# Two graph layers on one core: the third hop as seven products on layer 0's output, the fourth hop six tiles at once, the tests for the pattern in layer 0, first loads in another order

## The chip, the core and the metric

The kernel runs on one core of one Trainium2 chip. The core has TensorE (PE, matrix products), VectorE (DVE), ScalarE (ACT), GpSimd (POOL) and SyncE (SP, which here issues most of the DMAs). The metric is the device time of one execution in microseconds (us); lower is better.

## What is computed

N = 2048 nodes, B = 8 batches, C = 64 features, float32. `adj` is a row-normalised adjacency: each row has the same value at all its nonzero places, 1 over their number.

```python
# layer 0: Chebyshev terms I, A, 2AA-I, weights that depend on the node
w = jnp.einsum('nd,dkio->nkio', embedding, weight)      # D = 16, K = 3
x_g = jnp.einsum('knm,bmc->bnkc', A_stack, x)
out = jnp.einsum('bnki,nkio->bno', x_g, w) + b
x = _layernorm(x + out)
# layer 1: x0, then A x0 and 2 A A x0 - x0, twice with the same adj; one weight
out = jnp.einsum('bnf,fo->bno', x_cat, weight) + bias
x = _layernorm(x + out)
```

So there are four products with `adj`, called hops here: two for layer 0, two for layer 1.

## The kernel before

The nodes lie in 16 tiles of 128. `z[0]`, `z[1]` and `z[2]` hold three versions of the features, each 16 tiles of 128 x 512. A hop works on the pattern of `adj` (a matrix of ones and zeros) and multiplies by the row's value afterwards. The features go into TensorE in two parts, `high` (rounded, ACT) and `low` (the rest, DVE), so every block is multiplied twice. Pattern operands `s` are made from a slab `raw` of `adj`, by `places` (not equal to zero, L197) or by `places_equal` (equal to the row's value, L204), which also counts the places; the counts of the two tests are compared at the end (`check`), and where they differ a general kernel runs instead.

The stages, in the order of the code:

1. **First hop** (`hop_x`, L226): two groups of eight output tiles, 16 slabs each, 512 products of 128x128 by 128x512. ACT counts the places of each `s` by a copy `seen` in bf16 (L438). `put_together` (L390) makes sums of quarters of the pattern, which POOL stores in DRAM (`sums_of`). Ahead of it `first_constants` loads the first features and the bias table on ACT's queue, runs seven idle products and 32 small ones for the bias of each node (`pb`, L145).
2. **Second hop** (`seven_products`, L522): a recursion of one level, seven products of half the size in place of eight, 448 large products. Its result comes out transposed. ACT turns the stored sums into operands (L510); three of the seven products take a quarter of `adj` itself, loaded again and converted on DVE (L197). `put` adds the products together (L540).
3. **Layer 0** (`mix0`, `layernorm`, `project`): per node tile eight PSUM buffers `pm` of 12 products each (L339), 64 rows deep, in pairs that run beside one another; in the trace each of them leaves two records. DVE adds each `pm` to `acc` with the node's embedding as a scalar, four instructions a buffer (L345). Ahead of the last `pm` stand two groups of eight transposes (L265): that of the tile before, for its projection, and that of the next tile's `z[1]`. After the last `pm` comes `project` of the tile before (L358): three weight blocks side by side, 192 columns; ACT writes two of them to `z[0]` and `z[1]` (L365), DVE the third to `z[2]` (L366). `layernorm` goes through DVE (L303, L304), POOL (L306), ACT (L297), DVE (L298), ACT (L284), DVE (L286 to L292) and POOL (L309).
4. **Third hop** (`hop_h`, L226): groups of 4, 8 and 4 output tiles on the projected `z[0]`, 512 products, operands by `places_equal`; the result is added to `z[1]` (`evict`).
5. **Fourth hop**: eight output tiles at once (`hop_g`), then the other eight one by one (`hop_tile`), each followed by its layer norm and store.

The pool `psum` has four buffers of two banks, and all stages draw on it in turn: `bank(name)` takes the next one, whatever it is for. In layer 0 that makes 12 in each tile: seven `pm`, two `pt`, one `pm`, two `pu`. The DMAs and, where `in_order` is set, the work of ACT and DVE keep the order in which the code issues them. In layer 0 `in_order` is empty, and the order on each engine is that of a scheduler. `run` walks through the steps of the hops; each step has parts with a lead (loads four steps ahead, operands two steps ahead), and `todo` holds work of which two pieces follow each step.

Of the kernel before, what the change touches and what calls it, by code (L numbers as in the profile page):

```python
# [8 lines left out]
F32 = mybir.dt.float32  # L9
# [17 lines left out]
WARM = 7  # L27
# [10 lines left out]
def pattern(  # L38
# [20 lines left out]

    nc = tc.nc  # L60
# [13 lines left out]
    rowpool = pool(hops, "frow", 1, side="right")  # L74
    hpool = pool(hops, "fhl", HL, side="right")
# [23 lines left out]
    equal = keep.tile([P, 3 * NT], F32, tag="equal", name="equal")  # L99
# [13 lines left out]
    v = const.tile([P, 3, C], F32, tag="v", name="v")  # L113
# [4 lines left out]
    late_copies = []  # L118
# [7 lines left out]
    def first_constants():  # L126
        load(nc.scalar, z[0][0], x[0].rearrange("n b c -> n (b c)"))
        bias_sb = rawp.tile([P, N // 4 + C], F32, tag="raw", name="bias_sb")
        load(nc.scalar, bias_sb, bias)
        load(nc.scalar, rcol, rcols)  # L130
        eT, b0_sb = bias_sb[:, : N // 4], bias_sb[:, N // 4 :]
        pb = [bank("pb") for _ in range(2)]

        idle = spool.tile([P, 5 * P], BF16, tag="s", name="idle")
        nc.vector.memset(idle, 0.0)
        for _ in range(WARM):
            nc.tensor.matmul(pb[0][:, 0, :], lhsT=idle[:, :P], rhs=idle[:, P:], start=True, stop=True)
        nc.vector.memset(eps, EPS)
        nc.vector.memset(part, 1.0 / C)
        make_identity(nc, ident)  # L140

        for j in range(4):
            for g in range(4):
                q = slice(32 * g, 32 * g + D)
                nc.tensor.matmul(  # L145
                    pb[g // 2][:, g % 2, j * C : (j + 1) * C], lhsT=eT[q, j * P : (j + 1) * P], rhs=b0_sb[q],
                    start=True, stop=True, tile_position=(32 * g, 0),
                )
        for h in range(2):
            to = ebias[:, 8 * h : 8 * h + 8, :].rearrange("p (g t) c -> p g (t c)", g=2)  # L150
            late_copies.append((to, pb[h][:, :, : 4 * C]))

    wl = work2.tile([P, 5, C], F32, tag="t0", name="wl")

    loads = [(pack_sb, pack[:, : NT * D + C]), (wl.rearrange("p k o -> p (k o)"), pack[:, NT * D + C :])]
# [66 lines left out]
    def add_block(accs, s, hl, first, last):  # L222

        for i, a in enumerate(accs):
            for h in range(2):
                nc.tensor.matmul(  # L226
                    a, lhsT=s[:, i * P : (i + 1) * P], rhs=hl[h],
                    start=(first and h == 0), stop=(last and h == 1),
                )
# [3 lines left out]
    def run(steps):  # L233

        got = [{} for _ in steps]
# [64 lines left out]
    def layernorm(src):  # L300
# [8 lines left out]
        nc.gpsimd.tensor_tensor(xc, xc, wide(rsqrt(ss)), ALU.mult)  # L309
        return xc  # L310
# [7 lines left out]
    def mix0(t, tt, between):  # L318
# [4 lines left out]
        for g in range(2):  # L323
# [6 lines left out]
            for dg in range(D // DG):  # L330
                if g == 1 and dg == D // DG - 1:
                    between()
# [15 lines left out]
        return layernorm(acc)  # L348

    def project(t, hT, pus=None):  # L350


        for g in range(2):
            pm = bank("pu") if pus is None else pus[g]
            for i in range(2):
                for j in range(2):
                    q = slice(j * C, (j + 1) * C)
                    nc.tensor.matmul(  # L358
                        pm[:, j, i * 3 * C : (i + 1) * 3 * C], lhsT=hT[q, 2 * g + i, :], rhs=v[q],
                        start=True, stop=True,  # L360
                    )
            got = pm[:, :, : 6 * C].rearrange("p j (i k c) -> p j i k c", i=2, k=3)
            bs = slice(4 * g, 4 * g + 4)
            for s in range(2):
                nc.scalar.copy(bc(s, t)[:, bs, :].rearrange("p (i j) c -> p j i c", j=2), got[:, :, :, 2 - s, :])  # L365
            nc.vector.tensor_tensor(  # L366
                bc(2, t)[:, bs, :].rearrange("p (i j) c -> p j i c", j=2), got[:, :, :, 0, :],
# [12 lines left out]
    S1, S2, S4, S3 = range(4)  # L380
    couple = []
# [11 lines left out]
    def hop_x(g, kk, j):  # L393
        k = kk + KK * j

        def features(_):
            if g == 0 and k > 0:
                load(nc.sync, z[0][k], x[k].rearrange("n b c -> n (b c)"))

        def operands(got):  # L400
            if g == 0 and k == 0:

                s = got["s"] = spool.tile([P, 2, Q], F32R, tag="s", name="s")
                raws = [load_slab(adj[h, 0, :, :Q], [P, Q]) for h in range(2)]
                got["hl"] = halves(z[0][0])
                for h in range(2):
                    ordered(nc.vector.tensor_scalar(s[:, h], raws[h], 0.0, None, ALU.not_equal))
                for to, src in late_copies:
                    ordered(nc.vector.tensor_copy(to, src))
            else:  # L410
                raw = load_slab(adj[:, k, :, g * Q : (g + 1) * Q].rearrange("h m n -> m h n"), [P, 2, Q])
                got["s"] = places(raw)
                got["hl"] = halves(z[0][k])
            couple.append(got["s"])
# [12 lines left out]
        def use(got):  # L427
# [10 lines left out]
            ordered(nc.scalar.activation(seen, s, AF.Copy, accum_out=nonzero[:, i : i + 1]))  # L438
            if last and g == 1:
# [13 lines left out]
    def seven_products(s, to, more):  # L453
# [3 lines left out]
        sums, kept = [], {}  # L457

        def sum_of_y(kk, name):
# [11 lines left out]
            if name == "T2":  # L471
# [4 lines left out]
                return add(y, add(y, quarter(2, 2), quarter(1, 2), ALU.subtract), quarter(1, 1), ALU.add)  # L476
            y = xcpool.tile([P, BC], F32, tag="ln_xc", name="y")
            if name == "T4":
                return add(y, kept[kk // 2][:, kk % 2], quarter(2, 1), ALU.subtract)
# [3 lines left out]
        def step(p, kk):  # L483
# [5 lines left out]
            def y_high(got):  # L489
                hl = hpool.tile([P, 2, BC], F32R, tag="hl", name="hl")  # L490
                got["hl"] = [hl[:, 0], hl[:, 1]]
                if name[0] == "B":
# [6 lines left out]
            def load_sum(got):  # L499
                if isinstance(which, tuple):  # L500
                    return
                raw = got["raw"] = rawp.tile([P, 2, Q], BF16, tag="raw", name="raw")
                load(nc.sync, raw, sums_of[kk, :, :, which, :].rearrange("g m n -> m g n"))

            def operands(got):
                if isinstance(which, tuple):
                    got["s"] = places(slab(kk + KK * which[1], which[0] * HALF, HALF))
# [7 lines left out]
            def use(got):  # L515
# [3 lines left out]
                for i in range(2):  # L519
                    for h in range(2):  # L520
                        for c in range(2):
# [3 lines left out]
                            )  # L525
                if kk < KK - 1:
                    return
                if p < 6:
                    todo.extend([lambda: None] * 4)
                for i in range(2):  # L530
                    for c in range(2):
                        todo.append(lambda i=i, c=c: put(acc[i][:, c], i, c))
                todo.extend(more.get(p, ()))
# [21 lines left out]
            before = [(5, sum_y)] if name[0] != "B" else []  # L555
# [8 lines left out]
    def times_r(t):  # L564
# [6 lines left out]
    pieces = weights()  # L571
    more = {
        1: [lambda: ordered(next(pieces)) for _ in range(13)],
        5: [lambda: times_r(0), lambda: times_r(1)],
    }
    run([hop_x(g, kk, j) for g in range(2) for kk in range(KK) for j in range(2)] + seven_products(1, to_z2, more))
# [13 lines left out]
    def hop_h(g, first, n, k):  # L590
        def operands(got):
            if g == 0 and k == NT - 1:
                project(mixed[0], transpose(mixed[1].rearrange("p b c -> p (b c)"), "hT"))
                layer0.close()
                in_order.append(True)
            i = g * NT + k
            raw = slab(k, first * P, n * P)
            got["s"], got["hl"] = places_equal(raw, first * P, equal[:, i : i + 1]), halves(z[0][k])

        def use(got):  # L600
            s, hl = got["s"], got["hl"]
            if k == 0:
                accs[:] = banks(n)
            add_block(accs, s, hl, k == 0, k == NT - 1)
            if k == NT - 1:
                for i, a in enumerate(accs):
                    evict(z[1][first + i], first + i, a, i % 2)

        return [(2, operands), (0, use)]

    third = [hop_h(g, first, n, k) for g, (first, n) in enumerate(((0, 4), (8, 8), (4, 4))) for k in range(NT)]

    mixed = None
    tt = operands(0)
    for t in range(NT):
        done = {}

        def between():
            if mixed is not None:
                done["hT"] = transpose(mixed[1].rearrange("p b c -> p (b c)"), "hT")  # L620
# [5 lines left out]
        new = t, mix0(t, tt, between)  # L626
        tt = done.get("tt")
        if mixed is not None:
            project(mixed[0], done["hT"])
        mixed = new  # L630
# [27 lines left out]
    EARLY = 8  # L658
    late = []
    ks = [0, 1, 2, 3, 8, 9, 10, 11, 12, 13, 14, 15, 4, 5, 6, 7]  # L660
    hls = {}
    sums = keep.tile([P, 8, B], F32, tag="sums", name="sums")
    late_values = {}

    def hop_g(k):
        def operands(got):
            i = ks.index(k)
            if i == EARLY:
                hops.close()
            if i in (0, EARLY):  # L670
                late.append(pool(ctx, f"flate{i}", 1, reuse_waits="tile"))
            got["s"] = places(slab(k, 0, HALF))
# [3 lines left out]
        def use(got):  # L676
            s, hl = got["s"], hls[k]
            if k == ks[0]:
                accs[:] = banks(8)
            add_block(accs, s, hl, k == ks[0], k == ks[-1])  # L680
            if k == ks[-1]:
                for t, a in enumerate(accs):
                    evict(z[2][t], t, a, t % 2)

        return [(2, operands), (0, use)]

    def hop_tile(t, c):
        def operands(got):
# [3 lines left out]
            got["s"] = places(raw)  # L692

        def use(got):
# [13 lines left out]
            for o in (2 * t - 16, 2 * t - 15):  # L708
                if o < 8:
                    square_sums(bc(2, o), sums[:, o, :])  # L710
            if t == 11:
                late_values["scales"] = rsqrt(sums.rearrange("p t b -> p (t b)"))
            if t >= 12:
                for o in (2 * t - 24, 2 * t - 23):
# [9 lines left out]
    run(third + [hop_g(k) for k in ks] + [hop_tile(t, c) for t in range(8, NT) for c in range(2)])  # L724
# [324 lines left out]
```

## Time and profile before

| | |
|---|---|
| time, median of 3 runs | 839.27 us (838.78 to 840.99) |
| profiled execution | 841.55 us, its span 839.8 us, mean granted clock 0.996 |
| PE busy | 823.0 us (98%) |
| DVE busy | 607.4 us (72%) |
| ACT busy | 224.8 us (27%) |
| POOL busy | 128.4 us (15%) |
| DMA | 96.56 MB, 115 GB/s over the span |
| first hop | 7.97 to 127.0 us |
| second hop | to 228.56 us |
| layer 0 | to 594.21 us |
| third and fourth hop | to 828.46 us |

The span runs from the first to the last instruction; the execution's time also holds what lies around it (1.75 us here). The borders of the stages are read from the chain of waits. In the timeline each row is a start, a length, an engine, a line of the code, an operation, what it writes and reads, and how many instructions the row joins; in brackets is idle time of the engine just before it, and what ended it. A length ends when the result is written, so lengths of neighbours overlap a little, and the distance between starts says what an instruction costs its engine.

### The profile page before, as it was taken

How to read it: one execution, taken by the hardware profiler on the slowest of the kernel's cores; microseconds unless marked ns; L12 is line 12 of the kernel's file. 1: busy time of each engine (PE TensorE's matmuls, PEld its weight loads, DVE VectorE, ACT ScalarE, POOL GpSimd, SP SyncE). 2: the span in 40 equal slices, each digit the busy share in tenths (PEclk: the TensorE clock that was granted, in tenths of full speed). 3: DMA queues.
4: the chain of work that ended last, by engine and by line, in shares of the span. 5: the costliest groups of instructions: out<-in, count | busy, mean ns of one | idle time of the engine just before them, and what ended most of it. 6: DMA issues, size and time to landing. Idle time of an engine off the chain costs nothing.

```text
span 839.8 us, 14386 instructions
## 1 busy us (share of the span) xinstructions
PE 823.0 (98%) x5609; PEld 732.7 (87%) x5609; DVE 607.4 (72%) x1256; ACT 224.8 (27%) x427; POOL 128.4 (15%) x130
## 2 busy tenths in 40 slices
PE   8999999999999999999999999989999999999995
PEld 6888888888888999999999999989888878888884
DVE  5868758757877988888788888788867567534662
ACT  4445446773101111111111111111331132401210
POOL 0100000001641111111111110120101020102133
PEclk9999999999999999999999999999999999999998
DMA  9976786458400000000000000030256327544462
GB/s 327 399 237 197 234 288 202 145 152 280 126 14 3 13 14 14 14 14 14 14 13 14 14 13 14 25 102 2 75 182 192 93 73 245 172 140 123 136 179 92
DMA packets 57181, 96.56 MB, mean 115 GB/s; under 512 B 3984, under 2 KB 28816, under 8 KB 56976
## 3 DMA queue, kind: packets, MB, share of 16 engines
q1 hardware_dynamic: 52064, 82.39, 31.0%
q0 software_dynamic: 2304, 8.39, 3.1%
q10 hardware_dynamic: 2736, 4.76, 1.5%
q8 instruction: 47, 0.77, 0.4%
q14 instruction: 30, 0.25, 0.1%
HBM read 82.94 MB, written 12.58 MB: 114 GB/s over the span
## 4 chain that ended last, share of the span: by engine, by line
PE 93%; DVE 4%; DMA 1%; issue 1%; ACT 0%; POOL 0%; ACTq 0%; DVEq 0%; POOLq 0%
PE pm L339 35%; PE acc L226 35%; PE accT L522 12%; PE a L226 7%; DVE acc L345 3%; PE pu L358 2%; PE pt L265 1%; DMA raw<-in_adj 1%; DMA bias_sb<-in_bias 1%; DVE s L204 0%; POOL got L315 0%; PE pb L145 0%; ACT L284 0%; POOL xc L306 0%; DVE s L303 0%
## 5 line engine op out<-in xcount | busy, mean ns | idle before, releaser
L226 PE MATMUL acc<-hl,s 128*128 128x512 f32 x1280 | 294.8, 392 | 0.0
L226 PEld LDWEIGHTS acc<-hl,s 128*128 128x128 f32 x1280 | 241.7, 189 | 52.1 <-issue 0.8
L345 DVE SCALAR_TENSOR_TENSOR acc<-pm,pack_sb,acc 128x256 f32<-128x256 f32 x512 | 246.3, 483 | 41.2 <-PE pm L339 19.8
L339 PE MATMUL pm<-w,xt 64*128 64x256 f32 x1024 | 160.8, 378 | 3.9 <-DVE acc L345 3.8
L339 PE MATMUL pm<-w,t 64*128 64x256 f32 x1024 | 159.7, 376 | 0.2 <-ACT t L267 0.2
L339 PE MATMUL pm<-w,z 64*128 64x256 f32 x1024 | 159.6, 376 | 0.0
L339 PEld LDWEIGHTS pm<-w,xt 64*128 64x128 f32 x1024 | 107.8, 187 | 6.4 <-issue 3.3
L339 PEld LDWEIGHTS pm<-w,t 64*128 64x128 f32 x1024 | 110.5, 187 | 2.0 <-ACT t L267 0.6
L339 PEld LDWEIGHTS pm<-w,z 64*128 64x128 f32 x1024 | 110.4, 187 | 1.5
L197 DVE TENSOR_SCALAR s<-raw 128x1024 fp32r<-128x1024 f32 x87 | 67.4, 776 | 59.6 <-PE acc L226 49.7
L522 PE MATMUL accT<-s,hl 128*128 128x512 f32 x448 | 101.7, 389 | 0.0
L522 PEld LDWEIGHTS accT<-s,hl 128*128 128x128 f32 x448 | 84.1, 188 | 17.5
L208 ACT CAST hl<-z 128x512 fp32r<-128x512 f32 (+1 forms) x120 | 66.8, 578 | 116.5 <-PE acc L226 108.7
L212 DVE TENSOR_TENSOR hl<-z,hl 128x512 fp32r<-128x512 f32 (+1 forms) x120 | 81.5, 681 | 17.3 <-ACT hl L208 14.4
L204 DVE SCALAR_TENSOR_TENSOR s<-raw,rrow 128x512 fp32r<-128x512 f32 (+1 forms) x48 | 46.8, 978 | 26.3 <-PE acc L226 24.6
L267 ACT COPY hT<-pt 128x512 f32<-128x512 f32 x16 | 9.4, 585 | 204.4 <-PE pt L265 204.4
L306 POOL TENSOR_TENSOR xc<-acc,s 128x512 f32<-128x512 f32 x16 | 16.7, 1042 | 280.2 <-DVE s L304 280.2
L226 PE MATMUL a<-hl,s 128*128 128x512 f32 x256 | 58.5, 390 | 0.0
L226 PEld LDWEIGHTS a<-hl,s 128*128 128x128 f32 x256 | 48.0, 188 | 10.0
L255 POOL TENSOR_TENSOR z<-z,got 128x512 f32<-128x512 f32 x12 | 18.9, 1594 | 154.6 <-ACT got L254 154.6
L325 POOL TENSOR_TENSOR acc<-z,ebias 128x256 f32<-128x256 f32 x32 | 27.0, 865 | 85.9 <-ACT hl L208 84.3
L510 ACT CAST s<-raw 128x1024 fp32r<-128x1024 bf16 x32 | 33.6, 1051 | 12.0 <-ACT hl L208 11.3
(87 smaller groups left out, 476.1 us busy)
## 6 DMA issues: line engine op xcount, KB each, us to landing
raw<-in_adj SPq DMA_DIRECT2D x103, 512.0 KB, 4.5
raw<-in_adj SPq DMA_DIRECT2D x34, 256.0 KB, 3.0
sums_of<-z POOLq DMA_DIRECT2D x16, 512.0 KB, 4.6
raw<-sums_of SPq DMA_DIRECT2D x32, 256.0 KB, 2.8
xt<-in_xT SPq DMA_DIRECT2D x16, 256.0 KB, 2.6
out<-got ACTq DMA_DIRECT2D x16, 256.0 KB, 2.0
z<-in_x SPq DMA_DIRECT2D x15, 256.0 KB, 8.3
w<-in_w SPq DMA_DIRECT2D x3, 512.0 KB, 5.4
```

Of the source, the lines that this page charges most:

```text
L197: ordered(nc.vector.tensor_scalar(s, raw, 0.0, None, ALU.not_equal))
L204: ordered(nc.vector.scalar_tensor_tensor(s, raw, 0.0, r, ALU.add, ALU.is_equal, accum_out=count))
L208: ordered(nc.scalar.copy(to[0], src))
L212: ordered(nc.vector.tensor_tensor(to[1], src, to[0], ALU.subtract))
L226: nc.tensor.matmul(a, lhsT=s[:, i * P : (i + 1) * P], rhs=hl[h], start=(first and h == 0), stop=(last and h == 1),)
L255: ordered(nc.gpsimd.tensor_tensor(to, to, got, ALU.add))
L325: nc.gpsimd.tensor_tensor(part.rearrange("p (j i) c -> p j i c", j=2), bc(0, t)[:, 4 * g : 4 * g + 4, :].rearrange("p (i j) c -> p j i c", ...
L339: nc.tensor.matmul(pm[:, j, i], lhsT=tt[k][q, 2 * g + i, :], rhs=w[k][q, ds, :], start=(k == 0), stop=(k == 2),)
L345: nc.vector.scalar_tensor_tensor(part, pm[:, :, :, d, :].rearrange("p j i c -> p (j i) c"), emb_sb[:, t, dd : dd + 1], part, ALU.mult, ALU.add
L358: nc.tensor.matmul(pm[:, j, i * 3 * C : (i + 1) * 3 * C], lhsT=hT[q, 2 * g + i, :], rhs=v[q], start=True, stop=True,)
L510: ordered(nc.scalar.copy(s, got["raw"]))
L522: nc.tensor.matmul(acc[i][:, c], lhsT=hl[h][:, i * P : (i + 1) * P], rhs=S[:, c * 512 : (c + 1) * 512], start=(kk == 0 and h == 0), stop=( ...
```

## The change

- **First loads.** The two halves of the first slab are issued on SP first, then each `x` tile just ahead of its slab. The bias table moves to the `loads` list, loaded at the start of the first hop's second group; its products (`node_bias`) run in the second hop. Twelve idle products in place of seven. In the first step all products with `high` come ahead of those with `low`.
- **Quarters kept.** ACT stores every second `seen` tile, bf16, to `quarters` in DRAM. In `seven_products`, two of the three products on a plain quarter load it from there, and ACT converts it. The sums `T4` are made during the fourth product.
- **Tests in layer 0.** `test(t)`: a slab of the second half of `adj` is compared with the row's value and counted, one 1024-wide DVE instruction per tile ahead of the third `pm` (tile 8 has a second one ahead of its seventh; tile 15 has none, and issues operands of the third hop's first two steps).
- **Projection.** `layernorm` writes back to `z[0]`; `project` applies two weight blocks (128 columns).
- **Third hop.** `seven_products` on layer 0's output, into `zT` (transposed). The third weight block is applied to `zT` afterwards (`weigh`, 128 products of 64 columns) and the result is added to `z[1]` (`add_weighed`). The last tile is transposed and projected inside its first product.
- **Fourth hop.** Six output tiles at once in `hop_g`, operands by `places_equal` (768 wide); ten tiles one by one, the first two of them with `places_equal` as well.

```diff
-WARM = 7
+WARM = 12
...
     def first_constants():
         load(nc.scalar, z[0][0], x[0].rearrange("n b c -> n (b c)"))
-        bias_sb = rawp.tile([P, N // 4 + C], F32, tag="raw", name="bias_sb")
-        load(nc.scalar, bias_sb, bias)
         load(nc.scalar, rcol, rcols)
...
-    loads = [(pack_sb, pack[:, : NT * D + C]), (wl.rearrange("p k o -> p (k o)"), pack[:, NT * D + C :])]
+    loads = [(bias_sb, bias), (pack_sb, pack[:, : NT * D + C]), (wl.rearrange("p k o -> p (k o)"), pack[:, NT * D + C :])]
...
     def add_block(accs, s, hl, first, last):
 
-        for i, a in enumerate(accs):
-            for h in range(2):
...
+        order = [(i, h) for i in range(len(accs)) for h in range(2)]
+        if first:
+            order.sort(key=lambda ih: ih[1])
...
-    def layernorm(src):
+    def layernorm(src, to):
...
-        nc.gpsimd.tensor_tensor(xc, xc, wide(rsqrt(ss)), ALU.mult)
-        return xc
+        xc, r = (a.rearrange("p (g m) c -> p g m c", g=2) for a in (xc, wide(rsqrt(ss))))
+        nc.gpsimd.tensor_tensor(to, xc, r, ALU.mult)
...
     def project(t, hT, pus=None):
...
-                        pm[:, j, i * 3 * C : (i + 1) * 3 * C], lhsT=hT[q, 2 * g + i, :], rhs=v[q],
+                        pm[:, j, i * 2 * C : (i + 1) * 2 * C], lhsT=hT[q, 2 * g + i, :], rhs=v[q, 0:2, :],
...
+            nc.scalar.copy(z1_part, got[:, :, :, 1, :])
             nc.vector.tensor_tensor(
-                bc(2, t)[:, bs, :].rearrange("p (i j) c -> p j i c", j=2), got[:, :, :, 0, :],
+                z2_part, got[:, :, :, 0, :],
                 bias1.unsqueeze(1).unsqueeze(1).to_broadcast([P, 2, 2, C]), ALU.add,
...
     def hop_x(g, kk, j):
         k = kk + KK * j
 
-        def features(_):
-            if g == 0 and k > 0:
-                load(nc.sync, z[0][k], x[k].rearrange("n b c -> n (b c)"))
+        def features(got):
+            if g == 0 and k == 0:
+                got["raws"] = [load_slab(adj[h, 0, :, :Q], [P, Q]) for h in range(2)]
...
             ordered(nc.scalar.activation(seen, s, AF.Copy, accum_out=nonzero[:, i : i + 1]))
+            if j == 1:
+                ordered(nc.scalar.dma_start(out=quarters[kk, :, :, g, :], in_=seen))
...
             def operands(got):
-                if isinstance(which, tuple):
-                    got["s"] = places(slab(kk + KK * which[1], which[0] * HALF, HALF))
+                if which == (0, 0):
+                    got["s"] = places(slab(kk, 0, HALF))
                 else:
...
-    third = [hop_h(g, first, n, k) for g, (first, n) in enumerate(((0, 4), (8, 8), (4, 4))) for k in range(NT)]
...
+    def weigh(ts, pairs, bs):
+        for n, t in enumerate(ts):
+            to = columns(pairs, n, bs)
+            for i in range(2 * len(bs)):
+                for j in range(2):
+                    q, block = slice(j * C, (j + 1) * C), 2 * bs[0] + i
+                    nc.tensor.matmul(
+                        to[:, j, i * C : (i + 1) * C], lhsT=zT[t // 8, t // 4 % 2][q, t % 4, block * P : (block + 1) * P],
+                        rhs=v[q, 2, :], start=True, stop=True,
+                    )
...
+    third = seven_products(0, to_zT, sums3, {
+        (0, 4): [last_transposed],
+        (0, 5): [lambda: in_order.append(True)],
+        (0, 6): [last_projected],
+        4: half_weighed(1, 0), 5: half_weighed(0, 1),
+    }, wait=2)
...
+    def test(k):
+
+        raw = slab(k, HALF, HALF)
+        return lambda: tc.keep_in_program_order(
+            nc.vector.scalar_tensor_tensor(
+                raw, raw, 0.0, rrow[:, HALF:], ALU.add, ALU.is_equal, accum_out=equal[:, k : k + 1]
+            )
+        )
...
+        at = {(1, 3): [between]}
+        if t < NT - 1:
+            at[0, 2] = [test(t)]
+        else:
+            at[0, 1], at[0, 3] = [lambda: early(0)], [lambda: early(1)]
+        if t == NT // 2:
+            at[1, 2] = [test(NT - 1)]
+        mix0(t, tt, at)
...
-    EARLY = 8
+    G = 6
...
-            got["s"] = places(slab(k, 0, HALF))
+            got["s"] = places_equal(slab(k, 0, G * P), 0, equal[:, NT + k : NT + k + 1])
...
-    run(third + [hop_g(k) for k in ks] + [hop_tile(t, c) for t in range(8, NT) for c in range(2)])
+    run(third + [hop_g(k) for k in range(NT)] + [hop_tile(t, c) for t in range(G, NT) for c in range(2)], third_got)
```

## The prediction

> **What bounds the kernel now.** First the busy times and the chain of waits, for the engine that sets the end; then the chain in order of time, for stage borders; then the timeline of VectorE (DVE) and TensorE (PE) inside one tile of layer 0, where the change adds work.
>
> ```profile
> PE 823.0 (98%) x5609; PEld 732.7 (87%) x5609; DVE 607.4 (72%) x1256; ACT 224.8 (27%) x427; POOL 128.4 (15%) x130
> PE 93%; DVE 4%; DMA 1%; issue 1%; ACT 0%; POOL 0%; ACTq 0%; DVEq 0%; POOLq 0%
> ```
>
> The chain is nearly all PE. Its pieces give the stages: first hop 7.97 to 127.0 us, second hop to 228.56, layer 0 to 594.21, third and fourth hop to 828.46, tail to 839.8. DVE's 72% hides layer 0. One of its tiles, first on DVE, then on PE (start us, us, engine, line):
>
> ```profile
> 385.59 2.04 DVE L345 SCALAR_TENSOR_TENSOR acc<-pm,pack_sb,acc 128x256 f32<-128x256 f32 x4 [0.92 <-PE pm L339]
> 387.55 0.41 DVE L366 TENSOR_TENSOR z<-pu,pack_sb 128x256 f32<-128x256 f32 x1
> 387.88 0.68 DVE L303 TENSOR_REDUCE s<-acc 128x8 f32<-128x512 f32 x1
> 388.59 0.17 DVE L304 TENSOR_TENSOR s<-s,part 128x8 f32<-128x8 f32 x1
> 388.68 0.42 DVE L366 TENSOR_TENSOR z<-pu,pack_sb 128x256 f32<-128x256 f32 x1
> 390.64 0.69 DVE L298 TENSOR_REDUCE ss<-sq 128x8 f32<-128x512 f32 x1 [1.55 <-ACT sq L297]
> ...
> 392.52 14.73 DVE L345 SCALAR_TENSOR_TENSOR acc<-pm,pack_sb,acc 128x256 f32<-128x256 f32 x28
> ```
>
> ```profile
> 404.79 0.43 PE L265 MATMUL pt<-ident,xc 64*128 64x64 f32 x8
> 405.04 0.44 PE L265 MATMUL pt<-ident,z 64*128 64x64 f32 x8
> 405.29 0.68 PE L339 MATMUL pm<-w,xt 64*128 64x256 f32 x4
> ```
>
> A tile lasts 22.57 us. DVE is occupied for all but the 0.92 before the last product pm7: 28 additions at 14.73/28 = 0.526, so the sixth product (pm5) is drained at 392.52 + 24 x 0.526 = 405.14. PE starts pm7 at 405.29. There are four PSUM buffers, and two transposes lie between pm6 and pm7, so pm7 takes pm5's buffer: the ring is closed to 0.15 us[...]. DVE's 0.92 is no slack: it is the time in which PE makes pm7 after DVE has freed its buffer. The trace has a test of this, where extra DVE work fell into tile 14:
>
> ```profile
> 546.79 0.69 DVE L204 SCALAR_TENSOR_TENSOR s<-raw,rrow 128x512 fp32r<-128x512 f32 x1 [1.33 <-DMA raw<-in_adj]
> ...
> 549.41 1.53 DVE L204 SCALAR_TENSOR_TENSOR s<-raw,rrow 128x512 fp32r<-128x512 f32 x1 [0.20 <-DMA raw<-in_adj]
> ...
> 550.88 1.20 DVE L204 SCALAR_TENSOR_TENSOR s<-raw,rrow 128x512 fp32r<-128x512 f32 x1
> ...
> 552.01 1.20 DVE L204 SCALAR_TENSOR_TENSOR s<-raw,rrow 128x512 fp32r<-128x512 f32 x1
> ```
>
> The first with its wait added 1.95 us; the other three stretched the gap between L304 and L298 from 1.96 to 4.0, so 2.05 more: 4.0 in all. PE's transposes at 540.76 and 590.02 lie 49.26 apart where two tiles are 45.14: 4.12 lost. DVE work here costs its full length.
>
> **The Trainium skill.** TensorEngine Tiling (Array Packing), PSUM Bottleneck: tiling speeds up TensorE, not the evacuation of PSUM. The trace agrees: 64-row products in pairs, and DVE without room. Perfetto Trace Analysis, Optimization Strategy: a gap repeating on the engine that should be full can mean too few buffers; the 0.92 on DVE, in each tile at one place, is its twin here. TensorE: Matmul & The Clock Gate, Part 1: cold PE runs at 1.2 GHz until some 3.4 us of work. The seven idle products took 3.17 us (0.425 apart) and the first 15 of the first hop 6.44, against 0.227 each later.
>
> **The change part by part.**
>
> *Start.* SP issues the two adjacency pieces ahead of x, and the bias load, which the chain waits for until 5.94, leaves the front with its 32 small products (1.98 us). Twelve idle products end at 1.25 + 12 x 0.425 = 6.35; the operands should be there by about 5.5 (the first x was cast at 4.68, the pieces are issued 0.9 earlier). The hop starts 1.6 earlier. It lost 119.05 - 512 x 0.2268 = 2.9 to the cold clock; without the gap I take 1.9 of that as gained. The bias products return in the second hop at 32 x 0.031 (the 64-column pace of L265): +1.0. Sum -2.5, bounds -4.5 and -1. The 16 new stores of quarters from ACT add 36 GB/s to 319 in the first half of the hop, where DMA is 0.89 busy; buffers run ahead and PE never waits there, so nothing. If that cover goes, PE waits; 2 us at most. ACT pays 16 issues of about 0.45 in a hop where it is half idle. In the second and third hop ACT's copy (1.05) replaces DVE's (0.78) in two products; ACT then needs 1.45 of a step's 1.81: nothing. The y sums of T4 move earlier under the same cover.
>
> *Layer 0.* (a) A 1024-wide test per tile, on DVE's queue between the second and third product, ahead of pm5. L204's 1024-wide row starts at 640.40 and its successor at 641.55: 1.15. The slab for it is issued a tile ahead on SP. (b) In the compiled order both L375 (was L366) stand ahead of the reduction; before, the second lay inside the wait for ACT and was free: +0.34. Each of tiles 1 to 14 pays 1.49: 20.9. Tile 0 pays nothing: DVE waits about 0.5 for each of its products. The second test of tile 8 lies after pm5, beside PE's pm7: +0.3. (c) project narrows from 192 to 128 columns: 16 records from 0.081 to 0.055, 0.42 a tile; behind a ring that DVE closes it saves nothing. (d) Tile 14's loss and 0.34 in tile 8 go: -4.4. (e) Tile 15 has no test, but early operands of the third hop: eleven 256-wide instructions at 0.35 fill an idle 1.9 and add 2.0, two more and four conversions at 0.61 add 3.1, L375 0.34. It has one transpose fewer, so pm7 takes pm4's buffer and the 0.9 goes: against 22.32 now, +4.8. Sum 20.9 + 0.3 - 4.4 + 4.8 = **+21.6**.
>
> *Third and fourth hop.* 64 large products fewer (448 for 512) at 0.2268: -14.5. 128 products of 64 columns, two records each as for L339 (3072 for 1536): 256 x 0.0306, the pace of L265 with the same stationary shape, +7.8; above, 0.062 as the bias records (1.98/32), +15.9; below, 64 columns at the slope of L358 to L339, 0.027, +6.9. Last tile's projection -0.6. Six tiles at once instead of eight leaves 512 products. DVE has 1.6 of a 2.7 us step there. The last tile's normalised result, about 7 us after its last addition, is wanted after five steps (9.1): hidden, and if not, the transposes hold PE by the difference. Sum -7.3. The tail stays.
>
> Total -2.5 + 21.6 - 7.3 = **+11.8**. The profiled execution took 841.55 (span 839.8), giving 853.4; it stood 2.3 above the median of the runs, so I predict 839.27 + 11.8 = **851.1**.
>
> **Rivals.**
> 1. DVE has room in layer 0 and PE sets the pace (faster). Place: the ring at pm7. If the test fitted into the 0.92 and the waits for ACT (1.5), tiles would take 22.57 - 0.42: -2.5 - 6.3 - 4.4 - 7.3 = -20.5, 818.8. It decides once a tile's extra falls below 1.49 - 11.8/14 = 0.65. For it: tests stand at 72% DVE, and casts in tiles 2 to 5 did vanish in that wait. Against: the test stands ahead of pm5, not in the wait, and tile 14 paid in full. 0.08.
> 2. Half of it: (b) free and part of a test hidden, start and tile 15 at their good ends: near 839. 0.05.
> 3. More than forecast: tests stretch beside GpSimd to 1.5 as at 549.41 (+5), or the small products are paced as the bias records (+8): 856 to 859. 0.15, on my side.
> 4. The change isn't what it says: the compiled order shows the tests, 128 small products and 448 large ones, so none.
>
> **Numbers.** About 0.3% (2.5 us) can be told from no change. My forecast with rival 3 has 0.87, so slower 0.87, same 0.05, faster 0.08. Low: no (b), best start, easier tile 15: 851.1 - 4.8 - 2 - 3 = 841. High: rival 3, 859.
>
> **What would show it.** Right: transposes in layer 0 some 24.05 apart, PE waiting 1 to 2 us a tile for DVE ahead of pm7, layer 0 near 387 us long, third and fourth hop near 227. Wrong: spacing near 22.2 without waits on PE (rival 1); third hop longer than 110 with small products 0.06 apart (rival 3); a first hop that starts after 7 us or shows waits for DMA.

## The result, and the profile after

The change makes the kernel slower: 865.84 us (median of 4 runs, 865.01 to 866.33) against 839.44 us before (median of 4). The ratio is 1.0308, interval 1.0295 to 1.0321. The forecast had the direction (slower, 0.87) and less than half of the size: 851.1 us, with 859 as the upper end. The profiled execution of the kernel after took 865.87 us with a span of 863.6 us, 23.8 us more than the span before.

From the page of the kernel after, the busy times and then the shares of the chain of waits:

```profile
PE 830.1 (96%) x5806; PEld 728.9 (84%) x5806; DVE 603.0 (70%) x1311; ACT 267.5 (31%) x464; POOL 109.8 (13%) x121
...
PE 62%; DVE 25%; issue 8%; POOL 2%; ACT 2%; DVEq 0%; POOLq 0%
```

Two things are to be seen. DVE now holds a quarter of the chain, where it held 4%: layer 0 goes over to it. And PE is busy for 7 us more, although it was given less to do in large products (1920 for 1984); that line can't be explained by layer 0.

One tile of layer 0 after, from the timeline, first DVE, then PE:

```profile
403.98 3.15 DVE L353 SCALAR_TENSOR_TENSOR acc<-pm,pack_sb,acc 128x256 f32<-128x256 f32 x6
407.05 1.22 DVE L704 SCALAR_TENSOR_TENSOR raw<-raw,rrow 128x1024 f32<-128x1024 f32 x1
...
408.19 10.43 DVE L353 SCALAR_TENSOR_TENSOR acc<-pm,pack_sb,acc 128x256 f32<-128x256 f32 x20
419.52 1.52 DVE L353 SCALAR_TENSOR_TENSOR acc<-pm,pack_sb,acc 128x256 f32<-128x256 f32 x3 [0.90 <-PE pm L347]
...
424.77 0.69 DVE L306 TENSOR_REDUCE ss<-sq 128x8 f32<-128x512 f32 x1 [1.89 <-ACT sq L305]
```

```profile
414.60 0.69 PE L273 MATMUL pt<-ident,z 64*128 64x64 f32 x16
416.62 0.70 PE L347 MATMUL pm<-w,xt 64*128 64x256 f32 x4 [1.33 <-DVE acc L353]
```

The test (L704) occupies DVE from 407.05 to 408.19, 1.14 us. The wait for PE ahead of the last additions is still there (0.90, before 0.92), and PE now waits 1.33 in each tile for a buffer. The ring of the forecast is as it was, and the test lengthens it. The stages, from the starts of their first products:

| | before | after | difference | forecast |
|---|---|---|---|---|
| start, first and second hop, to layer 0's first product | 228.8 | 232.7 | +3.9 | -2.5 |
| layer 0 | 365.3 | 379.0 | +13.7 | +21.6 |
| third and fourth hop | 235.5 | 241.9 | +6.4 | -7.3 |
| tail | 10.1 | 10.0 | -0.1 | 0 |

So layer 0 is cheaper than forecast, and everything around it dearer. The first row is the clue: the first hop's 512 products are the same in both kernels, start 1.9 us earlier after the change, and end only 0.4 us earlier. Large products that nobody had touched ran at another pace. Here is PE in two stretches that hold nothing but large products (columns: stretch; its length, PE busy and number of instructions; granted clock; DMA share; GB/s), before and after:

```profile
140.00:220.00 80.00, 80.00 (x354) 1.00 0.63 198
...
770.00:830.00 60.00, 60.00 (x266) 1.00 0.47 141
```

```profile
140.00:220.00 80.00, 80.00 (x345) 1.00 0.47 150
...
770.00:830.00 60.00, 60.00 (x263) 1.00 0.59 178
```

The clock is full, no instruction waits, DMA moves less in the second hop, and still 345 products fit where 354 did. From start to start a large product took 0.2267 us throughout before; after, it took 0.2343 in the first hop, 0.2333 in the second and third, and in the fourth 0.2342 in one half of the products and 0.2268 in the other. Over the 1920 large products this is 11.5 us more than at the forecast's 0.2268.

### The profile page after: what moved, and what is told of

Read it like the earlier page. It is cut to its first block, busy times and chain, and to the rows that moved or that the text cites. A ratio compares the mean times of both kernels' runs of the same rounds, so it can differ in the third digit from the quotient of the medians.

```text
span 863.6 us, 14814 instructions
## 1 busy us (share of the span) xinstructions
PE 830.1 (96%) x5806; PEld 728.9 (84%) x5806; DVE 603.0 (70%) x1311; ACT 267.5 (31%) x464; POOL 109.8 (13%) x121
## 4 chain that ended last, share of the span: by engine, by line
PE 62%; DVE 25%; issue 8%; POOL 2%; ACT 2%; DVEq 0%; POOLq 0%
PE accT L546 24%; DVE acc L353 20%; PE acc L230 14%; PE pm L347 10%; PE a L230 6%; PE accT L230 5%; PE accT L656 2%; POOL xc L314 1%; DVE ss L306 1%; ACT sq L305 1%; DVE z L375 1%; DVE s L311 1%; PE first L134 1%; POOL got L323 0%; ACT ln_sd L292 0%
## 5 line engine op out<-in xcount | busy, mean ns | idle before, releaser
L546 PE MATMUL accT<-s,hl 128*128 128x512 f32 x896 | 211.1, 396 | 1.2 <-DVE z L375 0.8
L546 PEld LDWEIGHTS accT<-s,hl 128*128 128x128 f32 x896 | 167.6, 188 | 42.5 <-DVE z L375 1.2
L230 PE MATMUL acc<-hl,s 128*128 128x512 f32 x512 | 120.7, 397 | 0.0
L534 ACT CAST s<-raw 128x1024 fp32r<-128x1024 bf16 x96 | 100.9, 1051 | 51.8 <-ACT hl L210 36.8
L230 PEld LDWEIGHTS acc<-hl,s 128*128 128x128 f32 x512 | 96.5, 189 | 24.1 <-DVE z L438 0.5
L214 DVE TENSOR_TENSOR hl<-z,hl 128x512 fp32r<-128x512 f32 (+1 forms) x96 | 53.3, 562 | 34.7 <-ACT hl L210 31.9
L210 ACT CAST hl<-z 128x256 fp32r<-128x256 f32 (+1 forms) x96 | 47.3, 510 | 66.3 <-PE acc L230 32.9
L230 PE MATMUL accT<-hl,s 128*128 128x512 f32 x192 | 45.5, 395 | 0.0
L230 PEld LDWEIGHTS accT<-hl,s 128*128 128x128 f32 x192 | 35.8, 188 | 8.1
L453 ACT ACTIVATE seen<-s 128x1024 bf16<-128x1024 f32 x32 | 33.7, 1053 | 16.8 <-DMA quarters<-seen 16.8
```

The source lines that it names most:

```text
L210: ordered(nc.scalar.copy(to[0], src))
L214: ordered(nc.vector.tensor_tensor(to[1], src, to[0], ALU.subtract))
L230: nc.tensor.matmul(accs[i], lhsT=s[:, i * P : (i + 1) * P], rhs=hl[h], start=(first and h == 0), stop=(last and h == 1),)
L534: ordered(nc.scalar.copy(s, got["raw"]))
L546: nc.tensor.matmul(acc[i][:, c], lhsT=hl[h][:, i * P : (i + 1) * P], rhs=S[:, c * 512 : (c + 1) * 512], start=(kk == 0 and h == 0), stop=( ...
```

## The experiments

The theory of the pace came from addresses, which stand in the compiled programs and in no view of a profile. The pool `keep`, which lies first in SBUF, grew by 352 bytes (`v` moved in; `equal`, `sums` and the columns of its square root shrank), and all that lies to the left of the free space moved with it: the pattern tiles `s`, and those feature tiles `hl` of the fourth hop that lie on that side. The `hl` of the first three hops are laid from the right end and stayed. (A large product takes 128 columns of one and 512 of the other; `s` is the stationary one in the first and fourth hop, `hl` in the seven products. "Pair" below means the start addresses of both.) The first idea was the remainder modulo 64.

**e1, e2: 32 bytes.** One unused tile at the start of `keep`, in the kernel after (e1) and before (e2):

```diff
+    keep.tile([P, 8], F32, tag="pad", name="pad")
     rcol = keep.tile([P, NT], F32, tag="rcol", name="rcol")
```

> The changed kernel with one unused tile of 32 bytes per partition at the start of its first SBUF pool, so that the stationary tiles s of the large products lie at 32 modulo 64 bytes, as the moving tiles hl do; without it s lies at 0. No instruction is added or removed. Theory A (where stationary and moving operand stand at different remainders modulo 64 bytes, a large product takes .234 us in place of .2267): the large products of hops 1 to 3 go back to about .227 and those of hop 4 to about .228, 1408 products x .0070 + 384 x .0025 = -10.8, and with the same at other places up to -13.5 us: 852 to 855. Rival B (the large products are slow because of the new order of loads, or because the kernel is a longer one): no change, 865 to 866.

> The kernel before with the same 32 bytes, which puts its s at 0 modulo 64 bytes while the hl of hops 1 to 3 stay at 32. Theory A: its 1472 large products of hops 1 to 3 go from .2267 to about .234, +10.5 us, hop 4, whose moving tiles move along with s, stays: about 850. If the place of s alone decides and not the pair, hop 4 is slower too: +13.5, about 853. Rival B: no change, 839.

e1 took 863.91 us, ratio to before 1.0283 (1.0266 to 1.0300), so 2 us of the 11.5 came back. e2 took 848.76, ratio 1.0093 (1.0074 to 1.0112): 8.5 us lost by 32 unused bytes. The stretches again, e1 and then e2:

```profile
140.00:220.00 80.00, 80.00 (x346) 1.00 0.49 153
...
770.00:830.00 60.00, 60.00 (x264) 1.00 0.60 184
```

```profile
140.00:220.00 80.00, 80.00 (x345) 1.00 0.60 189
...
770.00:830.00 60.00, 60.00 (x267) 1.00 0.43 138
```

e2 settles that addresses do it: apart from them nothing differs from the kernel before, and the second hop has the pace of after, while the fourth hop, where `s` and `hl` moved together, kept 267. So rival B is out. But e1 was a miss: modulo 64 its pairs agree everywhere, and it stayed slow. Put beside each other, all the traces agreed on another number:

| kernel | `s` mod 256 | `hl` of hops 1 to 3 | pace | `hl` of hop 4 | pace |
|---|---|---|---|---|---|
| before | 224 | 224 | 0.2267 | 224 | 0.2267 |
| after | 64 | 224 | 0.2343, 0.2333 | 224, then 64 | 0.2342, 0.2268 |
| e1 | 96 | 224 | 0.2324 | 224, then 96 | 0.2325, 0.2274 |
| e2 | 0 | 224 | 0.2333 | 0 | 0.2268 |

**e5, e9: 160 and 256 bytes.** The same unused tile with 40 elements in the kernel after (e5), and with 64 in the kernel before (e9).

> The changed kernel with an unused tile of 160 bytes in place of the 32 of e1, so that s and every hl leave the same remainder modulo 256 bytes (224). In the traces so far each pair of equal remainders modulo 256 ran at .2267 to .2274 (before 224/224, e2's hop 4 0/0, after's second half of hop 4 64/64, e1's 96/96), each unequal pair at .2324 to .2342, e1's 96/224 too, which are equal modulo 64 and 128. Theory A2 (equal remainders modulo 256, or a multiple of it, decide): all 1920 large products at .2267, the 11.6 us that after's spend over that go: 854. Theory A1 (64 decides, and something else held e1 up): as e1, 864. Rival B: no change, 866.

> The kernel before with an unused tile of 256 bytes: s leaves 224 modulo 256 as the hl of hops 1 to 3 do, but modulo 512 s now leaves 224 and they 480. Theory M256 (the remainder modulo 256 decides): every large product stays at .2267, no change, 839 to 840. Theory M512 (modulo 512): the 960 of hops 1 and 2 and the 512 of hop 3 go to .232 to .234, +8 to +10, about 848.

e5 took 855.81 us, ratio 1.0188 (1.0167 to 1.0209): 10.0 us less than the kernel after, of the 11.5 that the pace should give back (in its trace the first hop starts 0.2 later and PE waits 0.7 for DVE in it). e9 took 839.58, ratio 0.9995 (0.9985 to 1.0005). The same stretch of the second hop and one of the fourth, e5 and then e9 (in e9 the fourth hop ends inside the last stretch):

```profile
140.00:220.00 80.00, 80.00 (x354) 1.00 0.51 158
...
770.00:830.00 60.00, 60.00 (x267) 1.00 0.56 172
```

```profile
140.00:220.00 80.00, 80.00 (x355) 1.00 0.61 194
...
770.00:830.00 60.00, 57.87 (x256) 1.00 0.46 137
```

Theory A2 holds: with equal remainders modulo 256 every large product is back at 0.227. e9 shows that 256 is enough, since modulo 512 its pairs differ. Why the memory or the array behaves so is not shown; no run here looks inside a product.

**e4, e10: what the small products cost.** In the kernel after, the 128 products of `weigh` leave 256 records. e4 takes half of the stationary columns, e10 half of the moving ones.

```diff
-to[:, j, i * C : (i + 1) * C], lhsT=zT[...][q, t % 4, block * P : (block + 1) * P], rhs=v[q, 2, :]
+to[: P // 2, j, i * C : (i + 1) * C], lhsT=zT[...][q, t % 4, block * P : block * P + P // 2], rhs=v[q, 2, :]    # e4
+to[:, j, i * C : i * C + C // 2], lhsT=zT[...][q, t % 4, block * P : (block + 1) * P], rhs=v[q, 2, : C // 2]    # e10
```

> The changed kernel with 64 instead of 128 stationary columns in each of the 256 small products that apply the weights in the third hop; this leaves out their term for half of the nodes. Theory L (loading 128 fp32 columns of a row group takes about .11 us, two row groups in turn, so .060 per product): half the columns, .030 to .035 per product, 15.2 goes to 8 or 9 us, -6 to -7: 859. Rival M (the price is that of the 64 moving columns in fp32, or a fixed one of each record): 15.2 stays, 865 to 866.

> The changed kernel with 32 instead of 64 moving columns in each of the 256 small products that apply the weights in the third hop; this leaves out their term for half of the features. Theory L (as in e4: loading 128 stationary columns in fp32 sets their price): 15.2 us stay, 865 to 866. Rival M (moving columns count as well, so that e4's saving was that of a smaller product as a whole): .030 to .045 per product, -4 to -7.5, 858 to 862.

From the timelines of PE, the first 64 records and the large products behind them, in the kernel after, in e4 and in e10:

```profile
695.05 3.79 PE L656 MATMUL accT<-v,zT 64*128 64x64 f32 x64
698.77 7.50 PE L546 MATMUL accT<-s,hl 128*128 128x512 f32 x31
```

```profile
694.29 2.08 PE L656 MATMUL accT<-v,zT 64*64 64x64 f32 x64
696.30 10.07 PE L546 MATMUL accT<-s,hl 128*128 128x512 f32 x42
```

```profile
695.70 3.76 PE L656 MATMUL accT<-v,zT 64*128 64x32 f32 x64
699.39 6.96 PE L546 MATMUL accT<-s,hl 128*128 128x512 f32 x22
```

From start to start 64 records take 3.72 us after, 2.01 in e4, 3.69 in e10: 0.058, 0.031 and 0.058 each. e4 took 858.64 us (1.0219, 1.0198 to 1.0239), 7.2 less than after; 256 x 0.027 is 6.9. e10 took 869.0 (1.0339, 1.0314 to 1.0364); in its profiled run the granted clock stood at 0.98 from 615 to 800 us, as an estimate 185 x 0.02 = 3.7 us, about the 3.2 by which it lies above after. So from 64 moving columns down to 32 the price hangs on the stationary columns and not on the moving ones, as theory L has it. The Trainium skill, "TensorE: Matmul & The Clock Gate", LDWEIGHTS, says that a load takes P / 1.2 ns for P columns, whatever the rows, which makes 107 ns for 128; Part 3 of the page adds that loads overlap with running products only where the row group differs. With two row groups side by side that is, as an estimate, 0.053 a record for 128 columns and 0.027 for 64; measured are 0.058 and 0.031, each some 0.005 above. The trace's own records of these loads last longer than the page's 107, 188 ns for 128 columns (after) and 135 for 64 (e4), but they lie 53 apart, as 64 / 1.2 would have it. The transposes (L273) have the same form by the profile, 64*128 by 64x64, and take 0.031 a record; their loads last 139 ns, nearly as short as those of 64 columns. Why a transpose loads faster is open.

**e3, e7: where a test can hide.** e3 moves it from behind the additions of the second product to the place in `layernorm` where DVE waits 1.9 us for ACT; e7 moves it behind those of the sixth product (`pm5`), beside which PE makes the last one.

```diff
-            at[0, 2] = [test(t)]
+            at["wait"] = [test(t)]      # e3: run in layernorm, behind L312
+            at[1, 2] = [test(t)]        # e7
```

> The changed kernel with the test of a tile of layer 0 (1.15 us of DVE) moved from between the additions of products 1 and 2 to the place in layernorm where DVE waits 1.9 us for ACT. Theory (layer 0 goes round the ring DVE addition, PE product, DVE addition, and each test lengthens it by its own time; in the wait it is free): the period of a tile goes from 23.71 back to 22.57, 15 x 1.14 = -17 us, about 849. If DVE's port, shared with POOL during layernorm, stretches the work there by .3 a tile: -12, about 854. Rival (DVE has room in the ring, so the +14.7 of layer 0 came from the order of products and weights): no change, 865.

> The changed kernel with the test of a tile in layer 0 moved behind the additions of product 5, beside which PE makes product 7; there DVE waits .9 us for PE a tile. Theory R (any DVE work inside the ring of additions lengthens the period by itself less the wait it fills): 1.15 - .9 = .25 a tile, period about 22.8, -13: 853. Rival (the wait of .9 is made by DVE's own earlier additions through the banks, so that it moves along): period stays 23.7, 866.

e3 took 865.95 us (1.0305, 1.0288 to 1.0322): nothing gained, the period went from 23.71 to 23.61. It looks like the rival's result, and is not. DVE and POOL in e3, then POOL in the kernel after:

```profile
398.94 1.22 DVE L706 SCALAR_TENSOR_TENSOR raw<-raw,rrow 128x1024 f32<-128x1024 f32 x1
...
401.75 0.69 DVE L306 TENSOR_REDUCE ss<-sq 128x8 f32<-128x512 f32 x1 [1.59 <-ACT sq L305]
```

```profile
399.16 1.89 POOL L316 TENSOR_TENSOR xc<-acc,s 128x512 f32<-128x512 f32 x1 [17.97 <-DVE s L312]
```

```profile
399.32 1.04 POOL L314 TENSOR_TENSOR xc<-acc,s 128x512 f32<-128x512 f32 x1 [18.92 <-DVE s L312]
```

The wait on DVE is ended by ACT, but what fills it first is POOL's subtraction; with the test beside it that takes 1.89 in place of 1.04, and DVE still waits 1.59 afterwards. The 0.85 goes straight into the ring, and 0.19 more is lost because the 28 additions take 14.73 again, as without a test among them, and not 14.54: of 1.14 that leaves a gain of 0.1 a tile. The Trainium skill has the rule, "SBUF — State Buffer", Who interferes with whom: a DVE instruction with two inputs in SBUF contends with a GpSimd instruction that reads SBUF; the test has two (`raw`, `rrow`), and the 0.85 agrees. The expectation of e3 had 0.3 for this.

e7 took 855.6 us (1.0183, 1.0156 to 1.0211), 10.2 less. The period is 22.91, so theory R holds. PE around the last product of a tile:

```profile
410.02 0.69 PE L273 MATMUL pt<-ident,z 64*128 64x64 f32 x16
411.24 0.70 PE L347 MATMUL pm<-w,xt 64*128 64x256 f32 x4 [0.54 <-DVE acc L353]
```

PE waits 0.54 for the buffer instead of 1.33, and DVE's own 0.90 is gone, since the test fills it.

**e8: no tests in layer 0.** e5 with the tests in the third hop, where DVE is half idle.

```diff
+    for k in range(NT):
+        at, to = divmod(9 + 2 * k, KK), divmod(11 + 2 * k, KK)
+        more3.setdefault(at, []).append(lambda k=k: load_test(k))
+        more3.setdefault(to, []).insert(0, lambda k=k: test(k))
```

> e5 with the 16 tests taken out of layer 0 and put into the third hop, one every second step of its seven products, each with its load two steps earlier; there DVE is busy 5 to 6 tenths. Theory (PE bounds hop 3, DVE has room): layer 0 back to a period of 22.57, -17, and nothing added: with A2 854 - 17 = 837, at or a little below before. Rival (the tests delay the additions that free the third hop's banks, or their loads the ones that products wait for): up to +18 in hop 3, 854.

It took 842.7 us (median of 20 runs; 1.0033, 1.0026 to 1.0041), 13.1 less than e5. Layer 0 shrank by 13.4 and the third and fourth hop stayed at 237.4, so the tests cost nothing there. Two rows of DVE in the third hop:

```profile
625.94 0.41 DVE L215 TENSOR_TENSOR hl<-y,hl 128x256 fp32r<-128x256 f32 x1
626.27 1.22 DVE L690 SCALAR_TENSOR_TENSOR raw<-raw,rrow 128x1024 f32<-128x1024 f32 x1
```

It missed the 837 by 5.7 us: e5 was already 1.8 above its own expectation, and the period became 22.76 and not 22.57, 2.7 over 14 tiles, and the expected 17 had counted 15 tiles that pay 1.14 for a test, where 14 do. In its tiles the 28 additions take as long as before the change; the 0.19 is the second L375 (here L376), which now lies ahead of the reduction (L312):

```profile
391.31 14.73 DVE L354 SCALAR_TENSOR_TENSOR acc<-pm,pack_sb,acc 128x256 f32<-128x256 f32 x28
```

**e6: the start alone,** in the kernel before.

```diff
-WARM = 7
+WARM = 12
...
+    loads = [(bias_sb, bias), (pack_sb, ...
...
+        if first:
+            order.sort(key=lambda ih: ih[1])
...
+        (0, 3): [lambda: node_bias(sums2[1]), ...
```

> The kernel before with the new start alone: adjacency ahead of features, bias terms moved into the second hop's first product, 12 warming products, products of the first block ordered by half; layer 0, the third and the fourth hop and all addresses of s and hl as before. Theory (the step of the forecast was right, and only the slower large products hid it): -2.5 (1.6 earlier, 1.9 of cold clock, +1.0 of bias in hop 2), about 837. Rival (the loads that now come later make a later wait): no change, 839 to 840.

838.95 us (median of 20 runs) against 839.8 (39 runs), ratio 0.9988 (0.9981 to 0.9995): a gain of 0.85 us, a third of the forecast. Its trace alone would have misled, for its span is 2.9 shorter than that of the kernel before. PE in the first hop's beginning, before, in e9 (whose instructions are those of before) and in e6:

```profile
8.00:10.00 2.00, 2.00 (x5) 1.00 0.86 268
10.00:12.00 2.00, 2.00 (x6) 1.00 1.05 389
12.00:14.00 2.00, 2.00 (x7) 1.00 1.05 399
```

```profile
8.00:10.00 2.00, 2.00 (x7) 0.56 0.90 291
10.00:12.00 2.00, 2.00 (x7) 0.59 1.04 402
12.00:14.00 2.00, 2.00 (x10) 1.00 1.05 397
```

```profile
8.00:10.00 2.00, 2.00 (x11) 1.00 1.05 398
10.00:12.00 2.00, 2.00 (x10) 1.00 1.05 389
```

In the trace on which the forecast rested, PE ran at little more than half its pace until about 14 us; in e9's until 12, with the hop starting at 7.17 instead of 7.90 and ending at 124.9 instead of 126.9. This is read off the numbers of products: the clock column shows it in e9 (0.56 and 0.59) and reads 1.00 in the trace of before. That one execution was 2 us slower at its start than e9's, and the forecast booked this as a gain of the change. e6 is the fastest kernel of the study, by 0.1% over before; which of its parts gave that is not separated.

## Why the prediction was right and wrong

**Right: the mechanism in layer 0.** DVE's 0.92 is no slack where the test was put, DVE work in the ring costs about its length, and nothing hides the test. The trace shows PE waiting 1.33 us in each tile ahead of the last product (forecast: 1 to 2), and e8 shows that without tests 13.4 us of layer 0 go. Rival 1 is out, and e3 and e7 show why no simple place was free: the wait for ACT is a wait for POOL, too, which the test holds up; only the 0.9 behind `pm5` takes it, and e7 got 10.2 back there, of the 13.1 that e8 gained by taking the tests out. (The forecast's own lines had that wait for ACT, 1.55, beside its sentence that DVE is occupied for all but the 0.92.)

**Mis-sized: layer 0, +21.6 against +13.7.** A tile of 1 to 14 pays 1.14 and not 1.49. e8 parts it: order (b) costs 0.19 (forecast 0.34), and the test 0.95 (forecast 1.15). The test itself has 1.14 in the trace; the rest comes back because the 28 additions take 14.54 in the tiles with a test, 14.73 without; why they do is not shown. This is -4.9 over 14 tiles. Of the other terms, (d) gave -3.9 for -4.4, and (e) +3.4 for +4.8 (tile 15 takes 25.76 where it took 22.32); the third hop starts 1.4 earlier against the last layer norm, for which the forecast had taken 0.6 off the third hop.

**Failed: the price of the small products.** The step took 0.0306 from the transposes with the same shape and put the sum at +7.8. They cost 0.059, 15.2 in all. That the transposes don't load as other products do stood in the profile of before (after the first stroke: busy us, mean ns of one load):

```profile
L358 PEld LDWEIGHTS pu<-v,hT 64*128 64x128 f32 x256 | 22.5, 187 | 0.4 <-ACT hT L267 0.4
...
L265 PEld LDWEIGHTS pt<-ident,xc 64*128 64x128 f32 x128 | 7.3, 138 | 1.1 <-issue 0.4
```

Rival 3 had this end (+8 above the forecast), for a wrong reason: the 0.062 of the bias records belongs to the slow start of that one execution (in e9's trace the same 32 records take 1.12 us, 0.035 each). The nearest true row was L358 with its 128 stationary columns, but extrapolated along the moving columns to 0.027 it led below. With few moving columns the price no longer falls: it is 0.081 with 192 (L358), 0.056 with 128 (L366 in the kernel after), 0.058 with 64 and with 32. So the third hop's saving of 64 large products, 14.5, is paid out again in small ones.

**Failed: a term that was not there.** The forecast priced every large product at 0.2268, because that was its pace throughout the trace of before, and so put the effect of the new addresses at nothing. The diff changes the size of a pool, and with it the remainder of `s` modulo 256: +11.5 us, of which e5 got 10.0 back. No view of the kernel before could show it; the compiled program's addresses could have raised the question, and only e2 and e5 answered it.

**Failed: the start,** -2.5 against -0.85 (e6), as above: the slow first products of one execution were booked as the kernel's. The forecast knew that this execution stood 2.3 above the median of the runs, and still added the whole gain read off it to the median.

The errors in their order: +11.5 addresses, +7.4 small products, -7.9 layer 0, +1.7 start, +1.2 for waits of the third hop's first product for layer 0's last additions and projection, which the trace names and the forecast left out, +0.6 for the last tile's projection, which went from layer 0 and not from the third hop. Together 14.5 of the 14.7 by which 865.84 lies above 851.1. The range ended at 859 because it was made of the ends of the terms that the forecast had; the largest error had no term.

Where the expected gain went: with the addresses mended and the tests out of layer 0 (e8), the change still stands 2.9 us above the kernel before. Its seven products save 14.5 and the weights cost 15.2.

## What to carry to other kernels

Ahead of any story about the changed part, compare the pace of an instruction that the change didn't touch: here it gave 11 us at a glance. Take the price of a new product from one with the same stationary columns and the same kind of operation, and see, in the records of its loads too, whether its load or its moving columns set it, before drawing a line through other sizes. An engine's wait is free room only if nothing that the wait stands for is held up by the new work: here POOL's subtraction was.

## What was not expected of the hardware

- A large product (128x128 by 128x512, fp32r) takes 0.2267 to 0.2274 us where the start addresses of its two operands in SBUF leave the same remainder modulo 256 bytes, and 0.2324 to 0.2343 where they don't, 2.5 to 3.4%; equal remainders modulo 64 and 128 alone (e1: 0.2324) don't restore it, unequal ones modulo 512 (e9) don't hurt. Other forms of product were not tested.
- 32 unused bytes made the kernel before slower by 0.93% (e2).
- POOL's subtraction takes 1.89 us in place of 1.04 beside a DVE comparison of two SBUF operands, and so 1.14 us of work put into a wait of 1.9 gained 0.1 a tile (e3).
- A transpose and a product of the same form differ: the load of 128 columns lasts 139 ns for the one and 188 for the other, and a record takes 0.031 and 0.058 us (L273 and L656 in the kernel after).
